# Latent attention in a fused attention and feed-forward kernel: scores from rounded halves of q and k placed by strided transfers, normalisation on ScalarE, and a range test by squares

## The chip, the cores and the metric

The kernel runs on one core of one Trainium2 chip. A core has a TensorE (PE in the profile) for matrix products, a VectorE (DVE), a ScalarE (ACT), a GpSimd (POOL) and a SyncE (SP), whose queue issues nearly all of this kernel's DMA transfers. Each engine runs its own instructions in order and waits for others by semaphores. The metric is the device time of one execution in microseconds (us), lower is better.

## The reference

The input is x, eight sequences of 1024 tokens with 256 features, in float32. The program first adds a causal latent attention to x and then a two-layer network with local attention and a gated feed-forward part (`_L0_ffn_ref`), which the change does not touch. The part concerned is:

```python
NH, HD, D_R = 16, 16, 32
x = _layernorm(x)                                   # no learned scale or shift
c_kv = x @ W_kv_down                                # (T, 128)
k_rope = _rotary_apply(c_kv @ W_k_rope, cos, sin)   # one for all heads
k = (c_kv @ W_k_up).reshape(Bb, Tt, NH, HD)
v = (c_kv @ W_v_up).reshape(Bb, Tt, NH, HD)
q = (x @ W_q).reshape(Bb, Tt, NH, HD)
q_rope = _rotary_apply(x @ W_q_rope, cos, sin)
scores = jnp.einsum('bqhd,bkhd->bhqk', q, k)
scores = scores + jnp.einsum('bqr,bkr->bqk', q_rope, k_rope)[:, None]
scores = scores / math.sqrt(HD + D_R)
scores = jnp.where(causal[None, None], -jnp.inf, scores)
w = jax.nn.softmax(scores, axis=-1)
attn = jnp.einsum('bhqk,bkhd->bqhd', w, v).reshape(Bb, Tt, D_MODEL)
return attn @ W_o                                   # added to the input
```

## The kernel before

The attention is the function `mla`; the network behind it is `local`. At the end a check of ranges decides whether a general, slower path has to run after all; with these inputs it doesn't.

The exponential of a score is split into a product. The rotary part of the scores is the same for all 16 heads, so `rotary` (line 402) forms exp of it once for each block of 128 keys and up to 512 queries and keeps it in the tile `er`. For each group of four heads `scores` (line 421) multiplies k and q on PE (line 429), ACT takes the exponential of the PSUM tile `sc` into `pt` (line 437), `turned` multiplies `pt` by `er` on DVE (line 451), and `values` (line 453) multiplies by v on PE into `acc` (line 462). v carries a column of ones, so the sums of the softmax come out with it. No maximum is subtracted; this is why ranges are checked: `rotary` takes a second exponential, of the negated scores, and both exponentials leave row sums in `most` and `least` (lines 407 and 409), which are compared with a bound after the last sequence (lines 621 and 622).

A head has 16 dimensions, and PE is used as four tiles of 32 rows side by side, one for each head of a group. `wq` and `wk` are copies of the weights with the columns reordered so that two heads share 32 rows. `query` (line 355) and `keys` (line 362) form q and k for all heads, a head pair in 32 rows. For k, ACT writes two copies (line 372), each multiplied by a column of `mask` that keeps one head of a pair and sets the other's rows to zero. All of it is float32. A matmul in float32 stands in the profile as two records of the same shape.

The work of a sequence is cut into 36 units, of four heads and 512 columns each (`units`, line 571). Twelve of them join two blocks at the diagonal, of 256 and 256 or 384 and 128 columns. A software pipeline goes through them: at step s PE forms the scores of unit s, ACT takes their exponentials, DVE multiplies unit s-1, and PE forms the values of unit s-2. Everything else, the layer norm (`statistics`, `normalise`, `turn`), the projections (`down`, `rope_q`, `rope_k`, `query`, `keys`, `value`), `rotary` and the output product (`out_add`), stands "beside" the units: the table `at` (from line 518) names for each step which pieces are issued after it, for this sequence, the one before or the next. The order on PE, DVE, ACT and POOL is this order written out (`manual_schedule`); no scheduler changes it there. Transfers on SP's queue stand in program order too.

The kernel divides eight PSUM banks: four hold the scores of one unit (`pscore`), two the two `acc` tiles, and two (`psum1`) serve everything beside. A score bank of unit s+1 can be written only when the exponentials of unit s have read it. `dense` (line 324) is the helper for the projections; it writes 128 rows as four quarters (`times`, line 198), so its matmuls have line 200 in the profile. `on_a` is a copy from PSUM on ACT (line 78). `rsqrt` is a power on POOL (line 125).

Of the kernel before, what the change touches and what calls it, by code (L numbers as in the profile page):

```python
# [29 lines left out]
F32 = mybir.dt.float32  # L30
AF = mybir.ActivationFunctionType
ALU = mybir.AluOpType
# [49 lines left out]
def preln_mla_local_kernel(  # L82
# [72 lines left out]
    def mla(ctx: ExitStack, verdict):  # L155
# [85 lines left out]
        wq = wp.tile([P, 2, 2, 4, 2, HD], F32, name="wq")  # L241
        wk = wp.tile([P, 2, 4, 2, HD], F32, name="wk")
        mask = wp.tile([P, 2], F32, name="mask")
        for e in range(2):
            nc.vector.tensor_reduce(
                mask[:, e : e + 1], ident.rearrange("p (r e d) -> p r e d", e=2, d=HD)[:, :, e, :], AX.XY, ALU.add
            )
        for m in range(2):
            for e in range(2):
                cols = slice(128 * m + 64 * e, 128 * m + 64 * e + 64)  # L250
                nc.scalar.copy(
                    wq[:, :, m, :, e, :], wqnat[:, :, cols].rearrange("p c (r d) -> p c r d", d=HD)
                )
                nc.scalar.copy(wk[:, m, :, e, :], wknat[:, cols].rearrange("p (r d) -> p r d", d=HD))
        wq = wq.rearrange("p c m r e d -> p c m (r e d)")
        wk = wk.rearrange("p m r e d -> p m (r e d)")

# [9 lines left out]
        most = wp.tile([P, B * 12], F32, name="most")  # L269
        least = wp.tile([P, B * 12], F32, name="least")  # L270

        class Batch:


            def __init__(self, b):
                self.b = b
                self.sums = {}
# [4 lines left out]
            def statistics(self, n, part):  # L282
# [17 lines left out]
                self.found.append((mv, rstd))  # L300

            def normalise(self, n, part):
                mv, rstd = self.found[n]
                if part == 0:
                    if n == 0:
                        self.xn = []
                    self.xn.append(p1.tile([P, 4, D], F32, tag="xn", name=f"xn{self.b}_{n}", bufs=3))
                xn = self.xn[n]
                for i in (2 * part, 2 * part + 1):
                    nc.vector.tensor_scalar(  # L310
                        xn[:, i, :], self.x[:, 4 * n + i, :], mv[:, i, 0:1], rstd[:, i : i + 1],
                        ALU.subtract, ALU.mult,
                    )
# [40 lines left out]

            def query(self, m, n, c, part=None):
                if m == 0 and n == 1 and c == 0 and not part:
                    self.q = of[self.b % 2].tile([P, 2, T], F32, tag="q", name=f"q{self.b}")
                ps = self.dense(f"psq{m}_", [wq[:, 0, m, :], wq[:, 1, m, :]], self.xnc, n, c, part)
                if ps is not None:
                    on_a(self.q[:, m, HALF[n]], ps)  # L360

            def keys(self, m, n, part=None):

                if n == 0 and not part:
                    if m == 0:
                        self.k = []
                    for e in range(2):
                        g = 2 * m + e
                        self.k.append(of[self.b % 2].tile([P, T], F32, tag=f"k{g}", name=f"k{self.b}_{g}"))
                ps = self.dense(f"psk{m}_", [wk[:, m, :]], [self.ckvT], n, 0, part)  # L370
                for e in range(2) if ps is not None else ():
                    nc.scalar.activation(
                        self.k[2 * m + e][:, HALF[n]], ps, AF.Identity, scale=mask[:, e : e + 1]
                    )

# [26 lines left out]
            def rotary(self, c, kb):  # L402
# [3 lines left out]
                n = 12 * self.b + 8 * (1 - c) + kb  # L406
# [1433 lines left out]
```

## Time and profile before

| what | value |
| --- | --- |
| median of 3 runs | 3347.74 us (3345.59 to 3348.41) |
| span of the profiled execution | 3347.4 us |
| first and last start of a score exponential | 36.6 us and 1003.2 us |
| score exponentials, L437 (x576) | 560.7 us busy on ACT, mean 1029 ns |
| multiplications by er, L451 (x576) | 674.8 us busy on DVE, mean 1217 ns |
| score matmuls, L429 (x3072 records) | 369.9 us busy on PE |
| value matmuls, L462 (x3072 records) | 332.9 us busy on PE |

The profile is of one execution. A row of the costliest groups gives line, engine, operation, what it writes and reads with the shapes, the count, then the busy time and the mean of one, and then the engine's idle time just before such instructions with what ended it. "Busy" for PE is modelled: matmuls overlap, and a mean of one is longer than the distance from one to the next. The views of windows give busy time by engine in a stretch, with the number of instructions. The chain is followed back from the last instruction to what released each piece of work.

### The profile page before, as it was taken

How to read it: one execution, taken by the hardware profiler on the slowest of the kernel's cores; microseconds unless marked ns; L12 is line 12 of the kernel's file. 1: busy time of each engine (PE TensorE's matmuls, PEld its weight loads, DVE VectorE, ACT ScalarE, POOL GpSimd, SP SyncE). 2: the span in 40 equal slices, each digit the busy share in tenths (PEclk: the TensorE clock that was granted, in tenths of full speed). 3: DMA queues.
4: the chain of work that ended last, by engine and by line, in shares of the span. 5: the costliest groups of instructions: out<-in, count | busy, mean ns of one | idle time of the engine just before them, and what ended most of it. 6: DMA issues, size and time to landing. Idle time of an engine off the chain costs nothing.

```text
span 3347.4 us, 79461 instructions
## 1 busy us (share of the span) xinstructions
PE 3270.7 (98%) x33826; PEld 1777.5 (53%) x33826; DVE 2686.0 (80%) x3993; ACT 1713.1 (51%) x2238; POOL 1341.6 (40%) x1031
## 2 busy tenths in 40 slices
PE   8999999999987899999999999999999999999998
PEld 2433333333333556666565666566666566665665
DVE  5888888888897887888878887777878778787773
ACT  6878878877862244434444434444444444344441
POOL 1000000000006655655655555555555555555540
PEclk9999999999998899999999999999999999999999
DMA  1000000000032444445344354444545444454431
GB/s 63 8 20 27 8 20 27 8 20 14 14 105 81 115 114 120 123 115 143 105 121 127 113 136 130 137 127 136 134 134 139 121 126 130 124 148 119 109 107 58
DMA packets 369290, 311.74 MB, mean 93 GB/s; under 512 B 154607, under 2 KB 333214, under 8 KB 368798
## 3 DMA queue, kind: packets, MB, share of 16 engines
q1 hardware_dynamic: 366942, 304.16, 33.1%
q8 instruction: 268, 4.39, 0.6%
q10 hardware_dynamic: 1984, 2.41, 0.2%
q14 instruction: 96, 0.79, 0.1%
HBM read 165.96 MB, written 140.51 MB: 92 GB/s over the span
## 4 chain that ended last, share of the span: by engine, by line
PE 90%; DVE 3%; ACT 2%; DMA 1%; issue 1%; SPq 1%; POOL 1%; ACTq 0%; DVEq 0%
PE ag L1088 17%; PE pair L859 13%; PE sc L429 9%; PE psy L1129 8%; PE acc L462 8%; PE psw L1005 7%; PE o L972 6%; PE pv L886 6%; PE pair L931 4%; PE psq L200 2%; PE psx L200 2%; PE s L980 2%; PE psR L200 2%; DVE pt L451 1%; PE psy L1135 1%
## 5 line engine op out<-in xcount | busy, mean ns | idle before, releaser
L451 DVE TENSOR_TENSOR pt<-pt,er 128x1024 f32<-128x1024 f32 x576 | 674.8, 1217 | 77.8 <-ACT pt L437 77.8
L437 ACT ACTIVATE pt<-sc 128x1024 f32<-128x1024 f32 x576 | 560.7, 1029 | 174.0 <-PE sc L429 161.6
L1088 PE MATMUL ag<-d,l 128*128 128x512 f32 x1408 | 640.4, 597 | 1.2 <-DVE xs L1009 0.8
L873 POOL TENSOR_TENSOR t<-t,t 128x1024 f32<-128x1024 f32 x128 | 302.0, 2360 | 792.0 <-DVE t L869 792.0
L937 ACT ACT_TABLE_LOAD x120 | 154.0, 1283 | 702.0 <-PE pair L931 702.0
L859 PE MATMUL pair<-l_qkv,xT 128*128 128x512 f32 x1024 | 469.2, 601 | 5.5 <-DMA xT<-zx 2.4
L1088 PEld LDWEIGHTS ag<-d,l 128*128 128x128 f32 x1408 | 262.2, 190 | 310.2 <-issue 278.1
L125 POOL TENSOR_TENSOR rn<-ss,half 128x16 f32<-128x16 f32 x128 | 373.4, 2917 | 13.7
L429 PE MATMUL sc<-q,k 32*128 32x512 f32 (+3 forms) x3072 | 369.9, 522 | 5.1 <-ACT pt L437 5.0
L462 PE MATMUL acc<-pt,v 128*32 128x512 f32 (+3 forms) x3072 | 332.9, 496 | 4.8 <-DVE pt L451 4.6
L859 PEld LDWEIGHTS pair<-l_qkv,xT 128*128 128x128 f32 x1024 | 193.7, 192 | 248.8 <-issue 207.6
L864 ACT ACTIVATE sq<-pair 128x1024 f32<-128x1024 f32 x128 | 131.0, 1023 | 333.2 <-issue 269.1
L866 DVE TENSOR_TENSOR t<-pair,l_cos 128x1024 f32<-128x1024 f32 x128 | 156.2, 1220 | 157.4 <-ACT sq L864 156.7
L1129 PE MATMUL psy<-l,hid 128*128 128x256 f32 x1280 | 281.5, 379 | 0.0
L1101 DVE SCALAR_TENSOR_TENSOR hid<-ag,l_b,ge 128x512 f32<-128x512 f32 x160 | 115.9, 724 | 196.3 <-ACT ge L1100 171.3
L1129 PEld LDWEIGHTS psy<-l,hid 128*128 128x128 f32 x1280 | 243.2, 190 | 46.7 <-issue 15.1
L937 ACT ACTIVATE pt<-pair 128x1024 f32<-128x1024 f32 (+1 forms) x256 | 234.9, 968 | 56.7 <-PE pair L931 55.4
L429 PEld LDWEIGHTS sc<-q,k 32*128 32x128 f32 x3072 | 157.3, 184 | 199.9 <-ACT pt L437 154.3
L411 POOL TENSOR_SCALAR_AFFINE_SELECT er<-er 128x128 f32<-128x128 f32 x64 | 51.5, 804 | 524.0 <-ACT er L407 524.0
L879 POOL TENSOR_TENSOR t<-t,rn 128x1024 f32<-128x1024 f32 x128 | 249.2, 1947 | 10.0
L972 PEld LDWEIGHTS o<-pt,v 128*32 128x32 f32 x7680 | 201.6, 110 | 88.0 <-issue 82.0
L886 PE MATMUL pv<-l_qkv,xT 128*128 128x512 f32 x512 | 240.6, 592 | 0.0
(132 smaller groups left out, 4876.8 us busy)
## 6 DMA issues: line engine op xcount, KB each, us to landing
z<-turned SPq DMA_DIRECT2D x512, 128.0 KB, 2.4
qkT<-z SPq DMA_DIRECT2D x128, 512.0 KB, 3.7
y<-xs SPq DMA_DIRECT2D x128, 128.0 KB, 2.6
h<-y SPq DMA_DIRECT2D x32, 512.0 KB, 4.0
zx<-turneds SPq DMA_DIRECT2D x120, 128.0 KB, 2.7
xT<-zx SPq DMA_DIRECT2D x240, 64.0 KB, 2.6
zh<-turnedh SPq DMA_DIRECT2D x120, 128.0 KB, 2.3
d<-zh SPq DMA_DIRECT2D x30, 512.0 KB, 3.2
```

What stands on the lines that cost most here:

```text
L125: nc.gpsimd.tensor_tensor(out_, in_, half[:, :n], ALU.pow)
L429: nc.tensor.matmul(two[n // 2][:, n % 2, lo : lo + w], self.k[g][rows, kb * P : (kb + 1) * P], self.q[rows, g // 2, q0 : q0 + w], start=Tr ...
L437: nc.scalar.activation(pt, sc, AF.Exp, scale=SCALE)
L451: nc.vector.tensor_tensor(t, t, er.to_broadcast([P, 1024 // w, w]), ALU.mult)
L462: nc.tensor.matmul(self.acc[g][32 * n : 32 * n + 32, q0 - c * 512 :], self.v[:, kb, h * VW : h * VW + 32], pts[n // 2][:, n % 2, lo : lo + w],
L859: nc.tensor.matmul(qk[:, n].rearrange("p h d -> p (h d)"), self.left(i)[c], w["qkv"][:, c, n * INNER : (n + 1) * INNER], start=(c == 0), s ...
L873: nc.gpsimd.tensor_tensor(t1, t1, t2, ALU.add)
L886: nc.tensor.matmul(pv, self.left(i)[c], self.w["qkv"][:, c, 2 * INNER :], start=(c == 0), stop=(c == 1))
L937: nc.scalar.activation(pt[:, :, : n * P], flat[:, :, : n * P], AF.Exp, scale=-1.0)
L972: nc.tensor.matmul(o[32 * j : 32 * j + 32, g, a, :], vs[m][:, h * DH + a * 32 : h * DH + a * 32 + 32], pts[m][g][:, place(j), off : off + ...
L1088: nc.tensor.matmul(ps.rearrange("p (s a t) -> p s a t", a=4, t=32), w["1"][:, c, i, :], d[:, c], start=(c == 0), stop=(c == 1),)
L1129: nc.tensor.matmul(ps[:, t, :], hid[:, i, cols], w["2"][:, i, :], start=(t == i == 0), stop=False)
```

## The change

Five edits are made in `mla`.

- **Halves.** `query` and `keys` use the weights as they are loaded; the reordered copies and the mask go. A new helper `halves` copies the PSUM result on ACT into a tile of type float32r, a float32 with a shortened mantissa, and on DVE subtracts this from the result, which leaves the remainder in the same type. The two together are the value.
- **Placement.** Transfers on SP's queue put the halves into the row order that PE wants: for q each row, with both halves behind one another, goes to two neighbouring rows; for k the first half goes to the even rows and the second to the odd ones. So each head again has 32 rows, all of them in use. q and k are kept in more, smaller tiles, most of them single.
- **Scores.** Each product is two float32r matmuls accumulated in PSUM, with the second and with the first half of q, over rows that hold both halves of k. The loop goes over the halves outside and over the four heads inside.
- **Normalisation.** The layer norm's scaling moves from DVE to ACT, as scale times x plus shift; two small POOL operations form the shift.
- **Range test.** The second exponential and the row sums go. Instead ACT squares the rotary q and k, four matmuls with ones sum the squares over the features, and one maximum on DVE for each sequence is kept.

The third buffers of `xn` and `onat` go. The core of the diff:

```diff
-        wq = wp.tile([P, 2, 2, 4, 2, HD], F32, name="wq")
-        wk = wp.tile([P, 2, 4, 2, HD], F32, name="wk")
-        mask = wp.tile([P, 2], F32, name="mask")
...
-        most = wp.tile([P, B * 12], F32, name="most")
-        least = wp.tile([P, B * 12], F32, name="least")
+        norms = wp.tile([P, B], F32, name="norms")
+        ones = wp.tile([P, 32], F32, name="ones_m")
+        nc.gpsimd.memset(ones, 1.0)
...
-                self.found.append((mv, rstd))
+                shift = small.tile([P, 4], F32, tag="shift", name=f"shift{b}_{n}")
+                nc.gpsimd.tensor_tensor(shift, mv[:, :, 0], rstd, ALU.mult)
+                nc.gpsimd.tensor_scalar(shift, shift, -1.0, None, ALU.mult)
+                self.found.append((shift, rstd))
...
-                    nc.vector.tensor_scalar(
-                        xn[:, i, :], self.x[:, 4 * n + i, :], mv[:, i, 0:1], rstd[:, i : i + 1],
-                        ALU.subtract, ALU.mult,
+                    nc.scalar.activation(
+                        xn[:, i, :], self.x[:, 4 * n + i, :], AF.Identity, scale=rstd[:, i : i + 1],
+                        bias=shift[:, i : i + 1],
                     )
...
+            def halves(self, ps, name):
+                t = p1.tile([P, 2, 512], F32R, tag="halves", name=f"{name}{self.b}", bufs=2)
+                on_a(t[:, 0], ps)
+                nc.vector.tensor_tensor(t[:, 1], ps, t[:, 0], ALU.subtract)
+                return t.bitcast(F32)
+
             def query(self, m, n, c, part=None):
...
-                    on_a(self.q[:, m, HALF[n]], ps)
+                t = self.halves(ps, f"qh{m}{n}_")
+                for g in (2 * m, 2 * m + 1):
+                    q = of[g % 2].tile([P, 2, 512], F32, tag=f"q{g}{n}", name=f"q{self.b}_{g}_{n}")
+                    for s in range(2):
+                        nc.sync.dma_start(q[s : P : 2], t[64 * (g % 2) : 64 * (g % 2) + 64])
+                    self.q[g, n] = q.bitcast(F32R)
 
             def keys(self, m, n, part=None):
...
-                for e in range(2) if ps is not None else ():
-                    nc.scalar.activation(
-                        self.k[2 * m + e][:, HALF[n]], ps, AF.Identity, scale=mask[:, e : e + 1]
+                t = self.halves(ps, f"kh{m}{n}_")
+                for g in (2 * m, 2 * m + 1):
+                    k = of[self.b % 2 if (m, n) == (0, 0) else 0].tile(
+                        [P, 512], F32, tag=f"k{g}{n}", name=f"k{self.b}_{g}_{n}"
                     )
+                    for s in range(2):
+                        nc.sync.dma_start(k[s : P : 2], t[64 * (g % 2) : 64 * (g % 2) + 64, s])
+                    self.k[g, n] = k.bitcast(F32R)
...
-                n = 12 * self.b + 8 * (1 - c) + kb
-                nc.scalar.activation(er, ps[:, :w], AF.Exp, scale=SCALE, accum_out=most[:, n : n + 1])
-
-                nc.scalar.activation(ps[:, :w], ps[:, :w], AF.Exp, scale=-SCALE, accum_out=least[:, n : n + 1])
+                nc.scalar.activation(er, ps[:, :w], AF.Exp, scale=SCALE)
...
+            def squares(self, n):
+                t = (self.rq, self.rk)[n]
+                sq = p1.tile([P, T], F32, tag="xn", name=f"sq{self.b}_{n}", bufs=2)
+                nc.scalar.activation(sq, t, AF.Square)
+                self.sq = getattr(self, "sq", []) + [sq]
+
+            def reach(self):
+                ps = bank(f"reach{self.b}")
+                for i, four in enumerate(QUARTER):
+                    nc.tensor.matmul(ps[four], ones, self.sq[i // 2][:, HALF[i % 2]], start=True, stop=True)
+                nc.vector.tensor_reduce(norms[:, self.b : self.b + 1], ps, AX.X, ALU.max)
...
-                    for n in range(4):
-                        rows = slice(32 * n, 32 * n + 32)
-                        nc.tensor.matmul(
-                            two[n // 2][:, n % 2, lo : lo + w], self.k[g][rows, kb * P : (kb + 1) * P],
-                            self.q[rows, g // 2, q0 : q0 + w], start=True, stop=True,
-                        )
+                    k = self.k[g, kb // 4][:, kb % 4 * P : (kb % 4 + 1) * P]
+                    q = self.q[g, c][:, :, q0 - c * 512 :]
+                    for h in (1, 0):
+                        for n in range(4):
+                            rows = slice(32 * n, 32 * n + 32)
+                            nc.tensor.matmul(
+                                two[n // 2][:, n % 2, lo : lo + w], k[rows], q[rows, h],
+                                start=(h == 1), stop=(h == 0),
+                            )
...
-            (22, 1, "query", 0, 1, 0, 1), (22, 1, "query", 0, 1, 1),
-            (23, 1, "keys", 0, 0), (23, 2, "statistics", 0, 0),
+            (22, 1, "query", 0, 1, 0, 1), (22, 1, "query", 0, 1, 1), (22, 1, "squares", 0),
+            (23, 1, "keys", 0, 0), (23, 2, "statistics", 0, 0), (23, 1, "squares", 1),
...
-            (26, 1, "keys", 0, 1), (26, 2, "statistics", 0, 1),
+            (26, 1, "keys", 0, 1), (26, 2, "statistics", 0, 1), (26, 1, "reach"),
```

In the built program the feed-forward part's first loads and statistics stand later against the last sequence's units than before, on SP's queue and on DVE; behind the last unit PE and ACT have the same order in both.

## The prediction

> **What bounds the kernel now.** I read the page's busy shares and slices first, then its costliest groups.
>
> ```profile
> PE 3270.7 (98%) x33826; PEld 1777.5 (53%) x33826; DVE 2686.0 (80%) x3993; ACT 1713.1 (51%) x2238; POOL 1341.6 (40%) x1031
> ...
> PE   8999999999987899999999999999999999999998
> ...
> DVE  5888888888897887888878887777878778787773
> ACT  6878878877862244434444434444444444344441
> ```
>
> The attention is the first twelve of the 40 slices (83.7 us each). The feed-forward part after it isn't touched. In these twelve PE is at 9, DVE and ACT at 8: three engines are nearly full, so what one gains another may take.
>
> ```profile
> L451 DVE TENSOR_TENSOR pt<-pt,er 128x1024 f32<-128x1024 f32 x576 | 674.8, 1217 | 77.8 <-ACT pt L437 77.8
> L437 ACT ACTIVATE pt<-sc 128x1024 f32<-128x1024 f32 x576 | 560.7, 1029 | 174.0 <-PE sc L429 161.6
> ...
> L429 PE MATMUL sc<-q,k 32*128 32x512 f32 (+3 forms) x3072 | 369.9, 522 | 5.1 <-ACT pt L437 5.0
> L462 PE MATMUL acc<-pt,v 128*32 128x512 f32 (+3 forms) x3072 | 332.9, 496 | 4.8 <-DVE pt L451 4.6
> ```
>
> Next the chain in order of time, in a steady sequence: it hardly leaves PE.
>
> ```profile
> 316.23 1.07 PE sc L429 x16
> 317.31 1.00 PE acc L462 x8
> 318.30 1.29 PE psq L200 x16
> 319.59 1.08 PE sc L429 x16
> ```
>
> One step is scores 1.07, values 1.00 and 0.86 or 1.29 of "beside" work, where a full 512-column product in quarters is 0.86. A sequence has 36 steps, 43 such products beside and 4 turns of 0.42: 36 x 2.07 + 43 x 0.86 + 1.7 = 113.2 us. The first score exponentials of three sequences start at 283.7, 405.0 and 526.3, a period of 121.3, so 8.1 are waits and starts. The windows (busy time by engine over stretches) give the others; the last two lines split one period into units 23 to 3 of the next sequence, and units 4 to 22:
>
> ```profile
> core 0: us, PE busy (x) PEld busy (x) DVE busy (x) ACT busy (x) POOL busy (x), PEclk, DMA share, GB/s
> 283.70:405.00 121.30, 120.30 (x1298) 47.21 (x1298) 107.67 (x138) 96.92 (x150) 9.49 (x10) 1.00 0.06 19
> ...
> 362.30:418.20 55.90, 55.90 (x636) 24.02 (x635) 50.63 (x70) 49.27 (x83) 4.74 (x5) 1.00 0.03 11
> 418.20:483.60 65.40, 64.40 (x668) 23.19 (x668) 57.03 (x69) 47.63 (x69) 4.76 (x5) 1.00 0.08 26
> ```
>
> DVE is idle 13.6 us of 121.3. That is the whole room of this change. What ends DVE's idle time in that sequence (waits):
>
> ```profile
> DVE pt L451 <- ACT pt L437: 7.6, 8, 2.1
> DVE rq L346 <- PE psrq L200: 2.4, 2, 2.3
> DVE x L508 <- PE psx L200: 2.3, 2, 2.0
> ```
>
> Rows by form that I price from:
>
> ```profile
> L372 ACT ACTIVATE k<-psk,mask 128x512 f32<-128x512 f32 x64 | 40.7, 693 | 0.5 <-PE psk L200 0.5
> L409 ACT ACTIVATE psR<-psR 128x512 f32<-128x512 f32 x48 | 29.9, 622 | 0.0
> L310 DVE TENSOR_SCALAR xn<-x,mv,rstd 128x256 f32<-128x256 f32 x64 | 23.1, 406 | 0.0
> L353 DVE TENSOR_TENSOR rk<-psrk,tab 128x512 f32<-128x512 f32 x16 | 11.1, 691 | 5.9 <-PE psrk L200 5.9
> ```
>
> **What the skill says.** (1) "FP8 and Floating Point Precision", TensorE Precision Notes: true FP32 takes four passes, the high and low products, while a reduced mode reads four bytes and truncates. The trace fits the first: in the scores two records of 512 columns follow at 0.427 us each, 0.853 = 4 x 512 columns at 2.4 GHz. The second is in no trace here. (2) "TensorE: Matmul & The Clock Gate", Part 3: matmuls on different row groups start about 4 ns apart and run together; a weight load costs its columns at 1.2 GHz. Here they start 7 ns apart, and 128-column rounds follow at 0.108 us. (3) "ScalarE: Activation LUTs", What ACT_TABLE_LOAD costs: 186 ns + 0.833 ns per element, about 93 more per pointer operand, 93 overlapped. L372 (one pointer, 693) against a 128x512 copy at 593 agrees.
>
> **The change part by part, per sequence.**
>
> Scores: as many matmul records as before (8 per unit and 512 columns), each one pass over half-width numbers. Taken: one column a cycle, so a round of four tiles is 0.213 instead of 0.427, and never under the 0.108 of a weight load. A unit falls from 1.07 to 0.21 + 2 x 0.213 = 0.64; a unit of 384+128 columns to 0.21 + 2 x 0.16 + 2 x 0.108 = 0.75. With 28 and 8 of them PE saves 38.5 - 23.9 = 14.6. Bounds of this unknown: nothing saved (a pass as slow as now), or, if the tiles didn't run together, a unit of 0.21 + 8 x 0.213 = 1.9. Neither is suggested by the f32 rows, so I take 0.64. New order: both halves of all four heads are interleaved, so no score bank is complete until both are free of the last unit's exponentials. With 1.00 of values and 0.86 beside between two score blocks and 1.94 for the two exponentials this costs nearly nothing; without work beside, up to 0.5.
>
> PE also gets the four range matmuls: one round, 0.86. PE's sum: 113.2 - 14.6 + 0.86 = 99.5.
>
> DVE loses 8 normalisations (23.1/64 = 0.36 each): -2.9. It gains 8 subtractions of a 128x512 PSUM tile, 0.69 like L353: +5.5, and a maximum over 128x512, taken like that row: +0.7 (bounds 0.4 to 1.2). DVE's sum: 107.7 + 3.3 = 111.0. By stretch: 50.6 + 4 x 0.69 + 0.7 = 54.1 against PE 45.5; and 57.0 - 2.9 + 2.8 = 56.9 against PE 53.9. **DVE becomes the bound in both.**
>
> The new waits are on DVE. A subtraction stands behind the multiplications of unit s-1, and needs the product beside unit s on PE and ACT's copy of it. When DVE leads, PE starts the values of s-2 as DVE ends their multiplication: 0.6 for their last half, about 1.2 beside, 0.2 signals, 0.6 copy, 0.2: 2.8 us, while DVE's two multiplications take 2.27 (the pitch at the end of the attention, where DVE is the bound). Each subtraction waits 0.5; eight make 4. Behind it stand the multiplications of unit s, and behind these PE's values. Bounds: 0 (the copy is early) to 1.2 each (the copy behind both exponentials). Period: 111.0 + 4.0 = 115.0, which is -6.3.
>
> ACT loses the second exponential of 12 range tests, with 24 accumulator reads, (49.6 + 43.2)/8 = 11.6, and a key copy each: 2.8. It gains 8 normalisations at 186 + 213 + 2 x 93 - 93 = 0.49 (an estimate from (3)), 3.9, and two squares of 1.04: 2.1. ACT goes from 96.9 to 88.5 of 115: off the path.
>
> Transfers: 32 issues a sequence on SP's queue, 6 MB in all, at 0.34 us an issue and 2.4 to 2.6 us to landing (128 and 256 KB rows). SP is nearly empty here; first use is 10 or more steps later, so they are hidden behind some 30 us. A staging buffer is reused after two steps at the soonest, 6 us against some 4.4 from the product to the landing. If that cover went, ACT's copy, and the exponentials behind it, would wait about 1 us at three places.
>
> Range test, masks, weight reordering, smaller pools: the reordering copies (2 us on ACT) fall away at the start while it waits; the output pool's third buffer is used on DVE alone, in order, so two cost nothing. POOL gets two small operations per statistics, hidden by 20 steps, except at the start.
>
> **Sum**, against the profiled 3347.4 (0.3 below the median of the runs): sequences 1 to 6: 6 x -6.3 = -38. Sequence 0 (125.8 now): its first step of 10.7 is ACT's burst of 16 exponentials, of which half go, PE's 7.5 remain: -3, and -4 later. Sequence 7: its first 14 units gain -3.5; then DVE already sets the pace. Start: +1.5 (two POOL operations, ACT 0.49 for DVE's 0.36). Hand-over: the first feed-forward statistics (8 BN, 8 aggregates) and scalings move on DVE from inside units 16 to 18 to behind the last multiplication, about -4 there and +4 in the tail: 0, give or take 6. Total -47: **3300 us**.
>
> **Rivals.**
> *DVE without waits*: 111.0 a period, 62 saved in six, with luck at the hand-over: **3268**. For it: stretches with 2.27 us a unit exist. Against: it waits for PE even now.
> *Longer waits on the new bound*: 0.8 to 1.2 us a subtraction, 117.5 to 120.5 a period: **3315 to 3340**. For it: ACT's queue is in order, with 1.94 us of exponentials ahead.
> *The pass isn't shorter*: units stay 1.07, PE 114.1, ACT's relief repays the 0.9: **3350**. For it: no trace here shows the mode.
> *Tiles don't overlap (slower)*: the four row tiles of the rounded type follow each other; PE's sum is 99.5 + 28 x 1.26 + 8 x 1.26 = 145, about 27 more than now with its waits: **3565**. It decides from 0.13 us a matmul, where a unit is 1.07 again. Against: every f32 record here starts 7 ns after its neighbour.
>
> **How the numbers follow.** Forecast 0.60 (its own range 3280 to 3315); no waits 0.08; longer waits 0.18, a quarter of it at or above no change; pass not shorter 0.08, half each within 0.2% and above; tiles 0.06. What this kernel's measurement can tell from no change is 0.2%, 6.7 us. Faster 0.60 + 0.08 + 0.135 = 0.81; same 0.03 + 0.04 = 0.07; slower 0.06 + 0.04 + 0.02 = 0.12. From 3264 to 3348 leaves out the slow cases and crumbs, about 0.2.
>
> **What would show it.** Score records of about 0.21 us a round, a unit near 0.64; DVE about 111 busy in a period near 115; waits of PE's values for DVE's pt instead of PE full; DVE waits named by the staging tile, near 0.5 each. The prediction is wrong if the period is 121 (pass or waits), if ACT waits for transfers, or if the tail after the last exponential (19 us now) grows by more than 6.

## The result and the profile after

The changed kernel takes 3316.48 us (median), the kernel before 3346.91 beside it: a ratio of 0.9908, with a 95% interval of 0.9894 to 0.9922. The forecast was 3300 with a range of 3264 to 3348. So the sign and the range hold, but the gain is 30 us where 47 were worked out. Between the two profiled executions it is 32.7 us (3347.4 to 3314.7), and it can be split at three marks, the first score exponentials of sequence 1, of sequence 7 and of the very last unit (this one, at 1003.2 us before, is the "last start" of the table above; the last exponential of all starts at 1004.1):

| stretch | forecast, us | measured, us |
|---|---|---|
| start and sequence 0 (to 162.3 before, 160.4 after) | -5.5 | -1.9 |
| six periods (121.33 each before, 118.01 after) | -38 | -20.0 |
| sequence 7, to the first exponential of its last unit (112.8, now 101.3) | -7.5 | -11.5 |
| the tail after it | +4 | +0.7 |
| sum | -47 | -32.7 |

(118.01 is the mean of six. Five of them are steady at 118.2; the sixth, in which three of the four statistics pieces are missing because no sequence 8 follows, takes 116.8.)

The page of the changed kernel, costliest groups (busy, mean of one | idle before it and what ended most of that):

```profile
L465 DVE TENSOR_TENSOR pt<-pt,er 128x1024 f32<-128x1024 f32 x576 | 672.0, 1221 | 10.8 <-ACT pt L451 10.8
...
L451 ACT ACTIVATE pt<-sc 128x1024 f32<-128x1024 f32 x576 | 559.6, 1027 | 117.1 <-PE sc L443 109.7
...
L476 PE MATMUL acc<-pt,v 128*32 128x512 f32 (+3 forms) x3072 | 384.4, 495 | 29.1 <-DVE pt L465 26.1
...
L443 PE MATMUL sc<-q,k 32*128 32x512 f32 (+3 forms) x3072 | 246.7, 381 | 10.2 <-ACT pt L451 9.6
```

The score products fell from 369.9 us busy to 246.7. The idle time ahead of DVE's multiplications fell from 77.8 to 10.8, and ahead of the values it rose from 4.8 to 29.1, ended by DVE: PE now waits for DVE, as forecast.

The windows, one steady period and then the same period cut at units 4 and 23 (busy time by engine):

```profile
core 0: us, PE busy (x) PEld busy (x) DVE busy (x) ACT busy (x) POOL busy (x), PEclk, DMA share, GB/s
278.70:396.90 118.20, 113.39 (x1306) 46.46 (x1304) 110.58 (x139) 93.13 (x120) 10.48 (x14) 1.00 0.29 73
```

```profile
292.74:354.03 61.29, 59.40 (x675) 23.45 (x677) 56.84 (x67) 49.26 (x64) 4.52 (x7) 1.00 0.30 79
354.03:410.99 56.96, 54.04 (x638) 23.05 (x632) 53.79 (x73) 43.91 (x57) 5.96 (x7) 1.00 0.27 66
```

DVE's sum is 110.6, forecast 111.0. But the period is 118.2, not 115.0: DVE is idle for 7.6 us, not for 4. And the whole gain is in the first of the two stretches: units 4 to 22 took 65.4 us before and take 61.3; units 23 to 3 took 55.9 and take 57.0, a little more. (PE's busy time now holds waits inside overlapping records. Its sum by pieces is about 100.5, an estimate: the forecast's 99.5 and 0.03 more for each of 36 score blocks.)

What ends DVE's idle time in that period (waits: us in total, times, longest):

```profile
DVE qh L348 <- ACT qh L79: 3.0, 3, 1.4
DVE kh L348 <- ACT kh L79: 1.4, 2, 1.1
DVE rq L332 <- PE psrq L201: 0.8, 1, 0.8
DVE x L522 <- PE psx L201: 0.8, 2, 0.4
DVE pt L465 <- ACT pt L451: 0.7, 1, 0.7
```

The first two lines are the eight subtractions, 4.4 us; the other three, 2.3 us, are waits that the kernel before had too.

The chain in order of time shows both regimes within one period. DVE first, around unit 3, then PE at units 7 to 9:

```profile
290.92 2.35 DVE pt L465 x2
293.28 0.60 DVE kh L348
293.88 0.35 DVE bnst L274
...
307.08 0.67 PE sc L443 x6
307.75 1.00 PE acc L476 x8
308.75 1.29 PE psx L201 x24
310.04 0.67 PE sc L443 x6
```

A unit of scores is 0.67 us (1.07 before, 0.64 forecast), and where 1.29 stands beside it a unit is 2.96 us instead of 3.36. Rows by form of the new operations, in that period:

```profile
L296 ACT ACTIVATE xn<-x,shift,rstd 128x256 f32<-128x256 f32 x8 | 4.4, 596 | 0.0
...
L348 DVE TENSOR_TENSOR qh<-psq,qh 128x512 fp32r<-128x512 f32 x4 | 2.8, 690 | 3.0 <-ACT qh L79 3.0
...
L348 DVE TENSOR_TENSOR kh<-psk,kh 128x512 fp32r<-128x512 f32 x4 | 2.8, 688 | 1.4 <-ACT kh L79 1.4
...
L425 DVE TENSOR_REDUCE norms<-reach 128x1 f32<-128x512 f32 x1 | 0.7, 683 | 0.0
```

These prices are as forecast: 0.69 for a subtraction, 0.68 for the maximum (0.7), and in the chain at the start seven normalisations on ACT take 3.54, so 0.51 each (0.49).

To see where a period changes, the pitch of each unit is useful: from the first score exponential of a unit to that of the next (median of sequences 1 to 5, us).

| unit | 0 | 3 | 5 | 8 | 10 | 12 | 17 | 19 | 22 | 28 |
|---|---|---|---|---|---|---|---|---|---|---|
| before | 3.71 | 3.36 | 3.90 | 3.36 | 3.36 | 4.51 | 3.36 | 3.36 | 3.36 | 3.05 |
| after | 3.72 | 5.01 | 5.70 | 2.96 | 3.84 | 3.71 | 2.96 | 2.96 | 3.76 | 4.18 |

Units 8, 9 and 17 to 21, where the chain runs over PE, are 0.4 shorter. Units 3, 5, 10, 22 and 28 are 0.4 to 1.8 longer; these five take back 5.5 us a period. In them, or up to two units ahead, stand the subtractions, the normalisations, the squares and the statistics.

### The profile page after: what moved, and what is told of

Same layout as the page of the kernel before. It is cut to its first block, busy times and chain, and to the rows that moved or that the text cites. A ratio compares the mean times of both kernels' runs of the same rounds, so it can differ in the third digit from the quotient of the medians.

```text
span 3314.7 us, 80062 instructions
## 1 busy us (share of the span) xinstructions
PE 3208.7 (97%) x33890; PEld 1772.6 (53%) x33890; DVE 2707.0 (82%) x3998; ACT 1683.3 (51%) x1990; POOL 1346.2 (41%) x1064
## 4 chain that ended last, share of the span: by engine, by line
PE 77%; DVE 12%; ACT 5%; issue 3%; DMA 2%; SPq 1%; POOL 1%; DVEq 0%; ACTq 0%
PE ag L1101 17%; PE pair L872 13%; PE psy L1142 8%; PE psw L1018 7%; PE o L985 6%; DVE pt L465 6%; PE pv L899 6%; PE acc L476 5%; PE pair L944 4%; PE sc L443 3%; ACT pt L451 2%; PE s L993 2%; PE psx L201 1%; PE psy L1148 1%; ACT pt L950 1%
## 5 line engine op out<-in xcount | busy, mean ns | idle before, releaser
L465 DVE TENSOR_TENSOR pt<-pt,er 128x1024 f32<-128x1024 f32 x576 | 672.0, 1221 | 10.8 <-ACT pt L451 10.8
L476 PE MATMUL acc<-pt,v 128*32 128x512 f32 (+3 forms) x3072 | 384.4, 495 | 29.1 <-DVE pt L465 26.1
L879 DVE TENSOR_TENSOR t<-pair,l_cos 128x1024 f32<-128x1024 f32 x128 | 156.2, 1221 | 156.0 <-ACT sq L877 155.3
L443 PE MATMUL sc<-q,k 32*128 32x512 f32 (+3 forms) x3072 | 246.7, 381 | 10.2 <-ACT pt L451 9.6
L1018 PE MATMUL psw<-l_o,oT 128*128 128x256 f32 x1024 | 241.1, 389 | 0.0
L985 PE MATMUL o<-pt,v 128*32 128x128 f32 x7680 | 237.0, 274 | 1.1 <-POOL pt L952 1.0
```

The lines of the kernel that those rows point to most:

```text
L443: nc.tensor.matmul(two[n // 2][:, n % 2, lo : lo + w], k[rows], q[rows, h], start=(h == 1), stop=(h == 0),)
L465: nc.vector.tensor_tensor(t, t, er.to_broadcast([P, 1024 // w, w]), ALU.mult)
L476: nc.tensor.matmul(self.acc[g][32 * n : 32 * n + 32, q0 - c * 512 :], self.v[:, kb, h * VW : h * VW + 32], pts[n // 2][:, n % 2, lo : lo + w],
L985: nc.tensor.matmul(o[32 * j : 32 * j + 32, g, a, :], vs[m][:, h * DH + a * 32 : h * DH + a * 32 + 32], pts[m][g][:, place(j), off : off + ...
L1018: nc.tensor.matmul(ps[:, i, :], oT[:, c, i * P : (i + 1) * P], self.w["o"][:, c, :], start=(c == 0), stop=(c == 3),)
```

## The experiments

The theories. **A**: the bound alternates inside a period: PE in units 7 to 22, DVE in units 23 to 6; only relief at the right place counts. **B**, the forecast's: DVE is the bound throughout, and its sum and waits make the period. **C**: transfers out of the two staging buffers hold ACT and DVE up. **D** and **E** come with single runs. All times below are medians; ratios are to the kernel before in the same runs. There the kernel before took 3348.0 to 3349.2, 1.1 to 2.2 more than beside the changed kernel, so a difference of medians between two experiments is good to about 2 us.

One more thing has to be read beside each profile, the clock that was granted to TensorE. It is 1.00 in the steady periods above, but each profile has short stretches at 0.50. In the kernel before, one of them lies in sequence 7 (the same columns as above, the clock is the last number but two):

```profile
952.70:959.50 6.80, 6.40 (x16) 1.40 (x20) 5.49 (x11) 3.20 (x4) 0.00 (x0) 0.50 0.46 140
```

The changed kernel has none up to its last exponential. Where a profile has more of them in the attention and a reading rests on it, it is said below, and there the steady periods, at 1.00, are the better comparison.

### 1. The same DVE work at another place (stats_moved)

```diff
- (3, 1, "statistics", 1, 1), ... (20, 2, "load"), ... (23, 2, "statistics", 0, 0),
- (26, 2, "statistics", 0, 1), ... (34, 2, "statistics", 1, 0),
+ (6, 2, "load"), ... (11, 2, "statistics", 0, 0), (12, 2, "statistics", 0, 1),
+ (15, 2, "statistics", 1, 0), (16, 2, "statistics", 1, 1),
```

> The changed kernel, with the load of x moved from unit 20 to unit 6 and the four statistics pieces from units 23, 26, 34 and 3 to units 11, 12, 15 and 16: the same DVE work, elsewhere in the period. Theory A (the bound alternates inside a period: PE in units 7 to 22, where DVE has some 4 us to spare, DVE in units 23 to 6): sequence 6 of the changed kernel already lacks three of the four pieces and is 1.4 us shorter, and unit 5 of sequence 7, without the fourth, 1.9: 3.3 us a period, about 20 in all, near 3296 (3293 to 3306). Theory B (DVE is the bound all through the period, as forecast; only its sum and its waits count): no change, 3316. Theory C (transfers out of the two staging buffers hold ACT and DVE up): no change, 3316.

Measured: 3311.95 (0.9888, 0.9872 to 0.9905), only 4.5 less than the changed kernel: outside A's range, and hardly below the 3316 of B and C. The period fell from 118.01 to 116.81; in the profiled execution six of them gave 7.2 us, and the stretch behind the last exponential took 3.6 back, for a reason that stays open. By units both halves of the answer are visible. What theory A counted on came: units 0, 5 and 25 to 28 lost 3.2 us. The pieces at units 11 and 12 cost nothing. But units 17 and 18 grew from 2.96 and 2.95 to 4.24 and 3.94, 2.3 us, because of the pieces at 15 and 16. The chain there:

```profile
321.75 4.53 DVE pt L465 x4
326.28 0.64 DVE onat L492
...
327.66 2.36 DVE pt L465 x2
330.02 0.66 DVE bnst L274 x2
330.68 0.22 DVE mv L276 x2
330.90 0.61 DVE onat L492
```

Around units 14 to 16 DVE already finishes two accumulators (the lines with onat, 1.38 us each with their reciprocals and products, beside 2.27 of multiplications a unit, where units took 2.6 to 3.3). The buffers between the engines carried that burst; with the pieces on top of it they didn't. So theory A's "DVE has 4 us to spare in units 7 to 22" was wrong as it was used: the 4 us are there as a sum, but at single units (10, 13, 18, 22), not wherever one likes.

### 2. The same move in the kernel before (before_stats)

> The same move of the load and of the four statistics pieces in the kernel before. There PE was busy 55.9 of 55.9 us in units 23 to 3, so DVE work taken from there should be worth little: theory A expects 0 to 5 us less than before, 3342 to 3347, well under what the same move gives after the change. Theory B expects no change either; if the gain is as large as after the change (15 us and more), theory A has the wrong reason.

Measured: 3342.01 (0.9978, 0.9967 to 0.9988), 6.0 us less than before, at the edge of what A expected: the period fell by 1.3, at units 0 (-0.35) and 5 (-0.97) alone. Here the pieces at units 15 and 16 cost nothing; a unit of 3.36 leaves DVE more room. At units 25 to 28 the move gives nothing before the change (3.04, 3.44, 3.46 and 3.05 stay) and 1.4 us after it: there DVE has become the bound, as A has it.

### 3. The subtraction one unit later (sub_later)

```diff
  on_a(t[:, 0], ps)
- nc.vector.tensor_tensor(t[:, 1], ps, t[:, 0], ALU.subtract)
+ # this and the transfers: behind the multiplications of the next unit
```

> The changed kernel, with each subtraction (and the transfers behind it) issued one unit later, behind the next unit's multiplications, so that it finds ACT's copy done. It costs nothing in work, but holds the product's PSUM bank a unit longer. Theory A: the subtractions wait 0.66 us each, 2.3 us a period in units 23 to 3 and 2.1 in units 4 to 22; only the first are on the bound: -2 to -3 us a period, about 15 in all, near 3301 (3298 to 3308). Theory B (DVE the bound everywhere): all 4.4 us a period, about 30 in all, near 3286. Theory D (the waits only took idle time that DVE has anyway, or the bank held longer makes PE wait): 3316 or more.

Measured: 3328.18 (0.9942, 0.9925 to 0.9958), 11.7 us more than the changed kernel, which is theory D's number. The waits of the subtractions are gone, and unit 28 fell from 4.18 to 2.77; but units 10 and 22, which had two of these waits, stayed within 0.01, so there DVE had only waited for what was late anyway. What theory A expected did come in units 23 to 3: they fell from 57.0 to 53.9. But units 4 to 22 rose from 61.3 to 65.2, most of it at units 3 to 5, where three products follow each other: 16.6 us instead of 14.4, with unit 4 alone at 9.2. In the timeline there (start, duration, in brackets the idle time before and its releaser):

```profile
295.90 0.58 ACT L79 CAST kh<-psk 128x512 fp32r<-128x512 f32 x1 [2.50 <-DMA q<-qh]
...
297.98 1.49 PE L201 MATMUL psq<-xnT,wqnat 128*32 128x512 f32 x8 [3.84 <-DVE kh L350]
```

ACT's copy waits for the transfer out of the staging tile, and PE for the PSUM bank that the late subtraction holds. A second cost comes with these stalls: 0.5 us after PE started again here, the clock was at 0.50.

```profile
298.50:301.90 3.40, 3.40 (x24) 0.91 (x20) 2.47 (x4) 1.24 (x2) 0.00 (x0) 0.50 0.69 154
```

In this stretch a block of scores took 1.16 us instead of 0.67 and one of values 1.52 instead of 1.00. Each of sequences 1 to 7 has such a stall, of 2.8 or 3.8 us, and beside it such a stretch, of 3.4 or once 6.8 us, while the steady periods of the changed kernel have none. So the loss at unit 4 is the stall and the slower clock with it. The cover that the forecast gave the staging buffer (some 6 us against 4.4) is real and is used up by one unit.

### 4. Every staging transfer twice (dma_twice)

```diff
- for s in range(2):
+ for s in (0, 1, 0, 1):
```

> The changed kernel, with every transfer out of the staging tiles issued twice (64 issues and about 12 MB a sequence). Theories A and B: transfers are hidden; the staging buffers are held some 2 to 5 us longer, which uses up the cover at the steps that follow each other closely (units 3, 4 and 5): 0 to 3 us a period, 3316 to 3340. Theory C (transfers hold up ACT and DVE already now): the waits grow by the whole of the added landing time at three or more places a period, 6 us a period and more, 3360 and above.

Measured: 3367.52 (1.0054, 1.0037 to 1.0071), 51 us more than the changed kernel. The range for A and B is missed, and the number lies where theory C put it; whether C's mechanism is there has to be read from the waits. ACT's, over the whole attention, here:

```profile
ACT kh L79 <- DMA k<-kh: 18.4, 8, 4.9
...
ACT qh L79 <- DMA k<-kh: 11.0, 6, 2.3
...
ACT kh L79 <- DMA q<-qh: 10.0, 3, 3.6
```

and in the changed kernel:

```profile
ACT kh L79 <- DMA q<-qh: 0.4, 1, 0.4
```

So theory C is wrong for the changed kernel, which loses 0.4 us to these transfers, and the forecast's "hidden" was right. But the cover is thin: with double traffic ACT waits 39.4 us for a staging buffer. Not all of the 51 us need be these waits: the clock was at 0.50 for 44 us of this attention, 27 of them at the start and in sequence 0, which together are 15.9 us longer; the two periods without such a stretch take 121.1 and 121.2, the four with one 121.7 to 124.7.

### 5. The parts undone one by one (norm_back, range_back, scores_back)

Each kernel is the changed one with one part as before: normalisation on DVE; the range test by second exponentials; the masked f32 scores.

> The changed kernel, with the eight normalisations a sequence back on DVE (and without the shifts on POOL). Theory B (DVE the bound): the whole 2.9 us a period come back, less what ACT's shorter queue gives (its two normalisations at unit 10 stand before the exponentials there, some 0.5); the start gets the 3.3 us back that it lost: 3316 + 7 x 2.5 - 3.3, near 3330 (3322 to 3334). Theory A (PE the bound in units 7 to 22): the six at units 4 to 6 count, the two at unit 10 don't: near 3326. If it is no slower than the changed kernel, DVE isn't what sets the period.

> The changed kernel, with the range test by a second exponential and two accumulator reads in each of the 12 rotary blocks, instead of squares, four matmuls and a maximum: ACT 93.1 to about 102.6 us a period, DVE -0.7, PE -0.9. Forecast and theory B (ACT is off the path): -0.7 to +0.5 a period, 3311 to 3320, of which sequence 0 has a burst of eight exponentials more, +3 to +5. Rival (ACT's queue is in order, and at 87% its waits reach the score exponentials, which DVE and PE wait for): 2 us a period and more, 3332 or above.

> The changed kernel without its score part: q, k, their masks and the four-pass score products as before, with the normalisation on ACT and the range test by squares of the change. Forecast (PE is the bound before, and only the shorter score rounds take work off it): PE's sum is 113.2 + 0.9 a period and the waits stay some 7 to 8: 3336 to 3352, no gain or little. Rival (undoing the range test cost 20.6 us and undoing the normalisation 5.5 of the 30 that the change gives, so the score part gives little by itself): 3320 to 3328.

| undone | median, us | ratio, interval | over the changed kernel: median, profiled span | period |
|---|---|---|---|---|
| normalisation | 3321.68 | 0.9919, 0.9899 to 0.9939 | +5.2, +3.6 | 118.66 |
| range test | 3337.05 | 0.9964, 0.9950 to 0.9978 | +20.6, +18.7 | 118.89 |
| scores | 3357.36 | 1.0026, 1.0016 to 1.0035 | +40.9, +39.5 | 121.50 |

(The first interval overlaps that of the changed kernel, and the time is below what A and B expected, 3326 and 3330.)

The scores are needed for any gain: without them the other two parts make the kernel 8 us slower than before. The three differences add up to 67, more than twice the gain of 30, but much of that stands in sequence 7, which is 7.3 us longer with the range test undone and 12.9 with the scores undone, each time with a clock of 0.50 for 10 to 14 us. In steady periods undoing the parts costs 0.7, 0.7 and 3.3, together 4.6, where the change gave 3.1: each part relieves what another loads, by half as much again and not by twice. DVE's 2.3 us of normalisation (110.6 to 112.9 busy) cost only 0.65 a period, because ACT's queue gets shorter by as much: unit 10, where two normalisations stand before the exponentials, falls from 3.84 to 3.01. The start gets 3.8 us back up to sequence 1 (156.6 for 160.4), of which the tail gives 3.2 up again.

The range test was expected near zero, with ACT off the path, and costs, between the profiled executions, 18.7 us: 4.7 up to sequence 1, 5.3 in six periods, 7.3 in sequence 7 and 1.5 behind it. Only the periods tell what ACT's work itself costs. The clock was at 0.50 for 10.2 us between 40.9 and 57.9 us, for 3.4 in the first period, which is 1.8 longer than the next, and for 13.6 between 945.4 and 965.8. In sequence 7 waits for loads of the feed-forward part's weights stand again too, 4.8 us on ACT and 6.3 on DVE. The windows of a steady period:

```profile
285.80:404.70 118.90, 112.98 (x1298) 46.68 (x1298) 109.86 (x138) 97.78 (x155) 11.91 (x14) 1.00 0.29 72
```

DVE has 0.7 less and PE 0.9 less to do, as the expectation said, and yet this period is 0.7 longer than the changed kernel's 118.2: ACT, with 97.8 of 118.9, isn't off the path. The rival's number, 3332 or above, came, but not its 2 us a period. ACT's busy time is 4.6 above the changed kernel's, not 9.5.

### 6. DVE's share and PE's share taken away (sub_pool, no_sub, one_pass)

The first has POOL subtract, from a second copy by ACT; the second leaves the subtraction out (low halves zero); the third leaves one score round out.

```diff
- nc.vector.tensor_tensor(t[:, 1], ps, t[:, 0], ALU.subtract)
+ on_a(whole, ps)                                               # sub_pool
+ nc.gpsimd.tensor_tensor(t[:, 1], whole, t[:, 0], ALU.subtract)
+ nc.gpsimd.memset(t.bitcast(F32)[:, 1], 0.0)                   # no_sub
- for h in (1, 0):
+ for h in (0,):                                                # one_pass
```

> The changed kernel, with the eight subtractions a sequence taken from DVE: ACT copies each product a second time (unrounded) into the staging tile, and POOL subtracts there in place. DVE loses 5.5 us of work and the 4.4 us that it waits in a period; ACT gains 8 x 0.6 = 4.8 (93.1 to 98); POOL, busy 10.5 us of 118, gains about 8 x 1.1. Theory B (DVE is the bound nearly everywhere: 110.6 us of work, 4.4 of waits for ACT's copies, 3.2 of other gaps): 6 to 10 us a period less, 3250 to 3276 (PE's own sum of 100.5 and its waits are next). Theory A (PE the bound in units 7 to 22): only the six subtractions outside these units count, some 5 a period, about 3280. Theory E (POOL and DVE keep each other off the SBUF, or the staging tiles are held so long that ACT waits for their transfers): 3300 or more.

> The changed kernel with the subtractions left out and the low halves set to zero by POOL (a write alone, some 0.5 us each; transfers and both score rounds stay). This takes the same 5.5 us of work and 4.4 of waits off DVE as the run with POOL's subtractions did, without POOL reading the SBUF beside DVE. If POOL's subtractions were slow only because the two engines kept each other off the SBUF (multiplications of up to 2.3 us instead of 1.22), this one shows what DVE's share is worth: theory B (DVE the bound nearly everywhere) 6 to 9 us a period, 3254 to 3275; theory A (PE the bound in units 7 to 22, DVE elsewhere) some 5 a period, near 3280. If it stays above 3300, neither: PE, DVE and ACT hand the wait on to each other, and no single engine's sum sets the period.

> The changed kernel with only one of the two score rounds (the product with the low half of q is left out; the halves are still made and moved): 28 x 0.21 and 8 x 0.16 to 0.21, some 7.5 us a period off PE. Theory B (DVE the bound): PE's share falls, but the time hardly does; only the gaps in which DVE waits for PE (2.3 us a period) can shrink: 0 to -2.3 a period, 3300 to 3316. Theory A (PE the bound in units 7 to 22): 16 units x 0.21 = 3.4 a period and more, 3292 or less.

sub_pool: 3324.63 (0.9928, 0.9912 to 0.9945), 8.2 us slower than the changed kernel, as theory E had it. The steady period, 118.35, is 0.1 longer (the profile has 6.8 us at a clock of 0.50 in sequence 0, which is 2.9 longer). DVE has eight operations fewer a period and is as busy as before, 110.1 us. Rows by form of a period:

```profile
L467 DVE TENSOR_TENSOR pt<-pt,er 128x1024 f32<-128x1024 f32 x73 | 89.7, 1282 | 4.8 <-ACT pt L453 4.8
L350 POOL TENSOR_TENSOR kh<-kh 128x512 fp32r<-128x512 f32 x4 | 7.4, 1859 | 14.2 <-ACT kh L79 14.2
```

The multiplications' mean rose from 1221 to 1279 ns over the whole attention, but not evenly: 39 of 576 took over 1.32 us, up to 2.32, where the changed kernel has none. The Trainium skill ("SBUF — State Buffer", SBUF: two separate sides) says that DVE and GpSimd share one pair of SBUF ports by an exclusive lock: of a DVE operation with two SBUF inputs and a GpSimd operation that reads the SBUF, the one that starts first has it for the whole instruction and the other is blocked. The records agree: a multiplication that started 0.07 us after a POOL subtraction of 1.29 took 2.30, and a subtraction that started 0.03 after a multiplication took 2.32, where the shortest take 1.26. It also says of the two ("Perfetto Trace Analysis", Optimizing Scalar/DVE Operations) that moving work between them might not help; here it didn't. The lock isn't the only cost of this run: ACT's second copies stand ahead of its exponentials too, and units 1, 10, 22 and 23, each with a copy, are 0.5 longer than in the changed kernel. no_sub has neither the copies nor POOL's reads.

no_sub: 3291.26 (0.9826, 0.9809 to 0.9842), 25.2 us less than the changed kernel; one_pass: 3295.05 (0.9843, 0.9826 to 0.9859), 21.4 less. The windows of a period, of no_sub cut at units 4 and 23, and of one_pass:

```profile
284.59:345.53 60.94, 59.16 (x676) 23.10 (x678) 55.10 (x63) 49.28 (x65) 8.82 (x12) 1.00 0.31 79
345.53:398.79 53.26, 51.53 (x638) 23.28 (x632) 50.58 (x69) 43.82 (x58) 6.21 (x10) 1.00 0.29 71
```

```profile
271.30:386.40 115.10, 107.06 (x1114) 40.65 (x1114) 110.42 (x139) 92.22 (x120) 10.96 (x14) 1.00 0.30 74
```

Taking 4.9 us of work and 4.4 of waits off DVE gives 3.8 a period, nearly all in units 23 to 3 (57.0 to 53.3); units 4 to 22 fall by 0.4. Taking a score round off PE, 7.5 us, gives 3.1, and here units 4 to 22 gain most (61.3 to 59.1, against 57.0 to 56.0). DVE's busy time stays at 110.4 while its idle time falls from 7.6 to 4.7. Theory B, with 6 to 9 for the one and 0 to 2.3 for the other, is out on both counts; A has the map right, but its numbers (near 3280, and 3292 or less) are missed too: neither relief pays in full.

### 7. Work moved to the gaps (tuned, tuned2)

Both also keep the first sequence's normalisation on DVE.

```diff
+ # tuned: statistics at 10, 11, 22, 26; load at 5; normalise(1, 1) at 8 instead of 10
+ # tuned2: statistics at 11, 12, 22, 26; load at 8; normalise at 4, 6, 7, 8
+ #         instead of 4, 5, 6, 10; squares(0) at 21 instead of 22
+ # both: the statistics at 22 and 26 stand ahead of the product whose subtraction waits
```

> The changed kernel with work moved to where the traces showed gaps: the statistics pieces at units 10, 11, 22 and 26, at 10, 22 and 26 ahead of the subtraction there, so that DVE does them while it waits for ACT's copy; the load at unit 5; the last two normalisations at unit 8, where ACT has 1 us to spare, instead of unit 10, where they stand before the exponentials; and the first sequence's normalisation on DVE, as before the change. Expected: 3.3 us a period from units 0, 5 and 25 to 28 as when the pieces were moved alone, but nothing given back at units 17 and 18, up to 0.8 from unit 10, 3 to 4 at the start: near 3289 (3284 to 3298). If DVE's sum and waits alone set the period, as theory B has it, the pieces in the gaps save at most the 2.5 us that DVE waits there: near 3298.

> The kernel of the run before (tuned), with what its trace showed late put right: there the first statistics piece, at unit 10, waited 2.8 us on DVE for the load of x, which started only at 302.5 us, unit 10 itself. Now the pieces are at units 11, 12, 22 and 26 and the load at unit 8; two normalisations leave unit 5, where they stood before the exponentials (at units 4, 6, 7 and 8 now), and the squares of rq leave unit 22 for unit 21, where ACT has 1 us to spare. Expected from the sum of the units: 2.4 us from units 11, 12 and 17, 0.8 each from units 5 and 22, a period of 112.3 instead of 116.3, about 24 us less than tuned: near 3277 (3272 to 3290). If DVE's sum and its waits for PE alone set the period (theory B), the moves on ACT give nothing: 114.0 or more, 3287 or above.

tuned: 3300.92 (0.9856, 0.9839 to 0.9872), 12 above its expectation and near theory B's 3298. A line of DVE's waits in one period says why: the load can't start before the last use of the buffer it takes. Five periods have such a wait, of 1.6 to 3.8 us, 11.6 in all.

```profile
DVE bnst L274 <- DMA x<-in_L_attn_x_dram: 2.8, 1, 2.8
```

tuned2: 3288.81 (0.9824, 0.9810 to 0.9837), 27.7 us below the changed kernel and 59.4 below the one before, in its range of 3272 to 3290 but 12 above its middle. Theory B named 3287 or above, so the time alone doesn't decide between them; the units do.

```profile
269.00:383.30 114.30, 112.10 (x1308) 46.98 (x1308) 110.12 (x139) 93.93 (x121) 12.66 (x14) 1.00 0.30 75
```

DVE and ACT have the same work as in the changed kernel, and the period fell from 118.01 to 114.16. The two moves on ACT gave the 0.8 each that they were put down for (unit 5 from 4.62 in tuned to 3.80, unit 22 from 3.76 to 2.95), where theory B has nothing to gain. Units 7, 16 and 17 are longer than summed, by 0.4, 0.3 and 0.5: unit 7 has one of the moved normalisations, the other two stay open.

## Why the prediction was right, and where its size went

**Scores.** Right. A unit takes 0.67 (0.64); one_pass puts the second round at 0.24 (2.96 to 2.72 at unit 19), for 0.21 forecast. The rivals "the pass isn't shorter" and "the tiles don't overlap" are excluded: the unit would be 1.07 or 1.9. That the new order, both halves of all heads interleaved, costs nearly nothing was argued, and no other order was run; what the page has is that the score products' waits for exponentials went from 5.0 to 9.6 us in the whole attention, under 1 us a period. (The price of a weight load that the forecast takes from Part 3 of the Trainium skill's "TensorE: Matmul & The Clock Gate" stands there in Part 2, LDWEIGHTS.)

**DVE's sum.** Right: 110.6 for 111.0, with each term as priced.

**The subtractions' waits.** Right in that period: 4.4 us in eight, 0.55 each for 0.5 (0.66 over all 64).

**The period, 111.0 + 4.0 = 115.0: the step that failed.** It measured 118.2. It took one engine's work and one new wait for the whole: DVE's idle time was put at 4.0 and is 7.6. Left out were 2.3 us of DVE's old waits for PE and ACT and 0.9 of short gaps. The reason behind it is "DVE becomes the bound in both", read from sums over stretches of 19 and 17 units. The unit pitches, no_sub and one_pass show that DVE's relief pays in units 23 to 3 and PE's mostly in 4 to 22, and stats_moved that the bound changes even from unit to unit: a sum over a stretch hides where each engine is late.

**ACT off the path: failed too.** The sum said 88.5; it measured 93.1. The mis-sized term is the range test: 11.6 us added up records that overlap. In the burst at the start of the kernel before, the chain gives one block of 512 columns, first its exponential and the accumulator's read, then the second exponential and its read:

```profile
35.39 0.69 ACT er L407 x2
36.08 0.60 ACT psR L409 x2
```

So the second exponential and its read take 0.60, where their records add up to 0.84, and the first read adds about 0.1; the twelve blocks, smaller ones among them, are some 7 us, which is what range_back's busy time says (4.6 and the squares' 2.2). And being idle for a fifth of the time didn't put ACT off the path: its queue is in order, and a normalisation or a square ahead of the exponentials delayed units 5, 10 and 22 by 0.8 each.

**Transfers.** Right that they are hidden (0.4 us of waits in all), and the warning beside it was right: sub_later and dma_twice show the cover gone, with waits of 2.5 to 4.9 us at one place instead of about 1.

**Start and sequence 0.** Forecast -5.5, measured -1.9. The start term was 1.5; norm_back is 4.2 earlier at its first score exponential (43.8 for 48.0) and 3.8 at that of sequence 1: at the start all eight normalisations follow each other on ACT, in front of everything. The other 1.3 us stay open.

**Sequence 7 and hand-over.** Forecast -3.5, give or take 6; measured -10.8. Units 16 to 18 took 17.2 us before and take 9.1. Only a part of that is the moved statistics. In the kernel before these waits stood there, in the window from 935 to 962 us:

```profile
DVE l_cos L686 <- DMA l_fcos<-in_L_ffn_k_scale_dram: 4.5, 1, 4.5
ACT pt L437 <- DMA l_qkv<-in_L_ffn_wqkv_dram: 4.5, 1, 4.5
...
ACT pt L437 <- DMA l_sin<-in_xpos_sin_dram: 3.2, 1, 3.2
```

After the change ACT's exponentials wait 1.3 us for such loads in all of sequence 7; with the range test back, it is 4.8 again. Whether the change does this through its queues or only by when the loads happen to be asked for is open: no run separates the two. The clock goes with it: in the kernel before, the 6.8 us at 0.50 begin when PE had stood idle for 3.2 us behind these waits, and units 18 and 19 run in them; at half speed they can account for up to 3.4 us (an estimate, if PE alone sets the pace there). Some 7 us of the measured gain lie here beyond the forecast. That they came was luck, and they hid part of what the periods fell short by.

The rival "longer waits on the new bound" named 117.5 to 120.5 a period and 3315 to 3340. The measured figures lie in it, but its mechanism doesn't: the subtractions wait 0.55, not 0.8 to 1.2.

## What to carry to other kernels

When three engines are each 80 to 95% busy, price a change unit by unit, by the pitch of one operation that each unit has, and not by sums over a stretch: slack is worth something only at the unit where it stands, and a buffered pipeline carries a burst but not a burst on top of another. Work on an engine that is off the path by its busy time still counts where it stands in the queue ahead of what the bound waits for; here moving pieces by one to fourteen units, and the first sequence's normalisation back to DVE, was worth almost as much again (28 us) as the change itself. Undo each part of a compound change in the finished kernel: here the score part has to be there for the others to pay. And look at the granted clock of each stretch before two profiles are compared.

## What the runs showed of the hardware that wasn't expected

- POOL subtracting two 128x512 tiles in SBUF took 1.26 us at the least and up to 2.35 beside DVE's multiplications, and these took up to 2.32 instead of 1.22.
- An accumulator read after an exponential has a record of 0.22 us, but moves the start of ACT's next operation by only 0.09: exponential (128x512) and read take 0.60 from start to next start, where the two records add up to 0.84.
- A strided transfer between two SBUF tiles lands after 2.4 us (128 KB) or 3.3 us (256 KB), and with twice as many of them after 2.4 and 3.7: the median landing time hardly grew, but ACT waited 39.4 us for the buffers behind them.
- TensorE's granted clock went to 0.50 for 3.4 or 6.8 us at or within 1.4 us behind each of seven stalls of PE of 2.8 to 3.8 us in sub_later's attention; a block of scores then took 1.16 us instead of 0.67. In the attention of all fourteen profiles 25 stretches at 0.50 begin. In the 3.4 us ahead of each, PE was busy for 0.01 to 0.64 of the time; other places where it was busy for only half of 3.4 us had none behind them, so a stall of PE can bring the lower clock, and when it does isn't settled here.
